# Two gated layers: order edges on the Sign activations and on the statistics of the next batch

## The chip, the cores and the metric

The kernel runs on one core of a Trainium2 chip. The metric is the device time of one execution in microseconds (us); the time before is a median of three executions.

## What is computed

The input is `x`, 4 batches of 512 tokens of width 512. Two layers follow one another, each of the same outer form:

```python
xn = layernorm(x)
x = x + attention(xn) * silu(ffn(xn))
```

In layer 0 the attention has 32 query heads of width 16 over 8 key heads, with a softmax over 512 keys; the ffn is a gated one, whose weights the kernel first multiplies with Hadamard matrices. In layer 1 the attention is a gated delta rule (a recurrence over the tokens, done in blocks), and the ffn uses only the signs of its weights:

```python
up_w, down_w = sign(up_weight), sign(down_weight)     # 2048x512, 512x2048
hidden = relu((x @ up_w.T) * up_scale)
out = (hidden @ down_w.T) * down_scale * output_scale
```

## The kernel before

**How an order comes about.** The source traces instructions engine by engine. A planner then writes each engine's stream at compile time: it plays the program through in a simulated time and lets, on each engine, the earliest instruction in the source's order go first among those that are ready in that simulated time. So an instruction whose inputs are ready early can stand far ahead of its place in the source. What a stream's order is once written, the engine follows: an instruction that waits holds back all behind it. The call `tc.keep_in_program_order(ins)` takes one piece of this freedom away: it adds an edge from the instruction that was traced last on the same engine to `ins`. The edge orders the two in the stream; it adds no semaphore and no wait.

**Layer 0.** One loop (`for u in range(NU + LATE)`, L529) runs over 256 units `u`, 64 for each batch. In unit `u` the attention does the row maxima of the scores of one pair of heads (`maxima`, two matmuls `sc` L402 on TensorE, one reduction `nmx` L403 on VectorE), and 11 units later the exponentials of the same pair (`exps`, two matmuls `st` L423, one activation `pe` L425 on ScalarE). There is one `sc` buffer and one `st` buffer (two PSUM banks each), so each unit's `st` matmuls wait until ScalarE has read the unit before, and each unit's `sc` matmuls until VectorE has. The ffn runs 16 units late (`v = u - 16`): of each 64 units the first 32 are the gate and up projections (`gate_up`, matmuls `mm` L316, then tanh L322 or a copy L326 on ScalarE), the other 32 the down projection (`down`, matmuls `y` L334). So gate_up stands in units 16 to 47, 80 to 111, 144 to 175 and 208 to 239, down in units 48 to 79 and so on. In batch 0 the weights are folded beside gate_up (`mix`, `fold`, `fold_down`; VectorE L52, L53, L247, L272); from batch 1 on they come back from memory, one 512 KB load `wc` (L312) for each unit, in 4 buffers.

**What else the loop places.** For the next batch: the load of `x` at unit 34 of each 64 (`load_x`, L128), four pairs `bn_stats`/`bn_aggr` at units 43 to 46 (`stats0`, L134 and L135), the standard deviation (`inv_std`, Sqrt L68 on ScalarE) and the normalization with its transposes at unit 49 (`norm0`, L73, L150 to L152). For layer 1: 32 tiles of weights, 256 KB each, are loaded into the three buffers `sn` (`load_weights`, L491 and L495, at units 100, 104, ... 224), turned into signs on ScalarE (`signs`, L498, at units 107, 111, ... 231) and stored to the memory tensor `sgn_d` (L499). Layer 1 reads `sgn_d` back from `load_signs` (L905) on.

```python
            if 100 <= u < 228 and u % 4 == 0:
                load_weights((u - 100) // 4)
            if 107 <= u < 235 and u % 4 == 3:
                signs((u - 107) // 4)
```

All DMAs of the loop are issued by one queue, SP's: `wc`, `sn`, `sgn_d`, `xin`, the small copies of queries (`qT` L389) and of the softmax denominators (`sum_d` L443, `rc` L445, `rec_d` L447, `sm` L450).

**Layer 1** begins after the attention's buffers are freed, some 818 us into the profiled execution.

Of the kernel before, what the change touches and what calls it, by code (L numbers as in the profile page):

```python
# [12 lines left out]
AF = mybir.ActivationFunctionType  # L13
# [20 lines left out]
def kernel(ctx: ExitStack, tc: tile.TileContext, i: dict, out: bass.AP):  # L34
    nc = tc.nc

    def new(pool, shape, dtype, tag, **kw):
        return pool.tile(shape, dtype, tag=tag, name=tag, **kw)
# [64 lines left out]
    if True:  # L103
# [20 lines left out]
        xins, xnTs, xrs = {}, {}, {}  # L124
# [5 lines left out]
        def stats0(b, t):  # L130
            if t == 0:
                lnp[b] = new(b0, [P, TB, 2], F32, "lnmv")
            s6 = new(b0, [P, 6], F32, "lnst")
            nc.vector.bn_stats(s6, xins[b][:, t, :])  # L134
            nc.vector.bn_aggr(lnp[b][:, t, :], s6)  # L135

        lnp = {}
# [79 lines left out]
        for t in range(TB):  # L217
            stats0(0, t)
# [276 lines left out]
                nc.sync.dma_start(sg, i["downT"][ts(c, P), :])  # L495

        def signs(n):
            nc.scalar.activation(sns[n], sns[n], AF.Sign)  # L498
            nc.sync.dma_start(sgn_d[n // 2, n % 2], sns[n])  # L499

        sns = {}
# [27 lines left out]
        for u in range(NU + LATE):  # L529
            b, r = u // 64, u % 64  # L530
# [30 lines left out]
            if 107 <= u < 235 and u % 4 == 3:  # L561
                signs((u - 107) // 4)
            if b + 1 < NB:
                if r == 34:
                    load_x(b + 1)
                if r in (43, 44, 45, 46):
                    stats0(b + 1, r - 43)
                if r == 49:
                    norm0(b + 1)
                if r == 52:  # L570
                    keys_values(b + 1)
# [712 lines left out]
    b = NB - 1  # L1284
# [20 lines left out]
    n = 0  # L1305
# [56 lines left out]
```

## Time and profile before

| | us |
|---|---|
| median of three executions | 1576.54 (1574.84 to 1581.1) |
| the profiled execution | 1569.52 |
| its span on the core | 1567.8 |
| TensorE busy / VectorE / ScalarE / GpSimd | 1474.4 / 1023.9 / 644.8 / 363.4 |
| mean granted TensorE clock | 0.978 |

The share of busy time is of the span. The page's 40 slices are 39.2 us each. In views of waits a row reads: who waited, on which line, for whom; then microseconds in total, how many times, and the longest. In a timeline a row reads: start, duration, engine, line, operation, tiles, shape, count, and in brackets the idle time before it and what ended it. An index of time that this document uses often is the unit: the k-th `nmx` reduction (L403) on VectorE is that of unit k, so its start says when unit k is reached. In the profiled execution unit 48 starts at 186.8 us, 80 at 286.5, 112 at 382.9, 144 at 471.0, 176 at 569.1, 208 at 657.2 and 240 at 750.1.

### The profile page before, as it was taken

To read this page: it belongs to the slowest core of one execution; us is meant where nothing else is said; L and a number is where in the kernel's file an instruction comes from. 1 tells how busy PE (TensorE), PEld (TensorE's weight loads), DVE (VectorE), ACT (ScalarE), POOL (GpSimd) and SP (SyncE) were. 2 spreads that over 40 slices of the span, in tenths; PEclk is the share of its full clock that TensorE was granted. 3 is DMA by queue.
4 is the path that set the end of the run, shared out by engine and by line. 5 is a ranking of instruction groups with operands and counts; after the bars stand their busy time and mean duration, and the time that the engine had idled before them with its cause. 6 is when DMAs were issued, how large, how long until landed. Compare 5 with 4: busy or idle time off the path is not lost.

```text
span 1567.8 us, 22716 instructions
## 1 busy us (share of the span) xinstructions
PE 1474.4 (94%) x8144; PEld 879.0 (56%) x8144; DVE 1023.9 (65%) x1805; ACT 644.8 (41%) x913; POOL 363.4 (23%) x354
## 2 busy tenths in 40 slices
PE   6999999999999999999998999998999999998896
PEld 2556533465335543456334666886578756875683
DVE  6899645765557655566517669568955897477553
ACT  4655655575446654466433423213231223121112
POOL 1112100322003210133101431154214521244023
PEclk9999999999999999999999999999999999999987
DMA  8856745375105631166014443424452435225513
GB/s 277 324 196 225 259 151 173 126 248 175 25 21 200 221 122 26 59 212 213 19 45 138 123 132 96 127 85 128 128 165 61 141 103 167 78 70 171 142 32 104
DMA packets 192512, 215.91 MB, mean 138 GB/s; under 512 B 66480, under 2 KB 129424, under 8 KB 191504
## 3 DMA queue, kind: packets, MB, share of 16 engines
q1 hardware_dynamic: 189648, 213.33, 43.0%
q10 hardware_dynamic: 2752, 1.14, 0.3%
q8 instruction: 64, 1.05, 0.3%
q14 instruction: 48, 0.39, 0.1%
HBM read 155.22 MB, written 54.58 MB: 134 GB/s over the span
## 4 chain that ended last, share of the span: by engine, by line
PE 64%; DVE 20%; DMA 7%; issue 3%; POOL 2%; ACT 2%; SPq 1%; POOLq 0%; ACTq 0%; DVEq 0%
PE y L334 14%; PE mm L316 10%; PE y L934 5%; PE ph L921 5%; PE sc L402 4%; PE pu L766 3%; PE pu L714 3%; DVE nmx L403 2%; PE po L435 2%; DVE UT L1023 2%; DVE sx L1019 2%; DVE yc L722 2%; PE mm L243 2%; PE pu L1120 2%; PE pu L1144 2%
## 5 line engine op out<-in xcount | busy, mean ns | idle before, releaser
L403 DVE TENSOR_REDUCE nmx<-sc 128x2 f32<-128x1024 f32 x256 | 312.3, 1220 | 151.4 <-PE st L423 128.0
L425 ACT ACTIVATE pe<-st 128x1024 f16<-128x1024 f32 x256 | 262.8, 1027 | 148.0 <-PE st L423 146.6
L334 PE MATMUL y<-wdn,hT 128*128 128x512 f32 x512 | 256.7, 622 | 4.9 <-DVE g L338 4.0
L316 PE MATMUL mm<-xr,wc 128*128 128x512 f32 x768 | 206.3, 409 | 0.9 <-DVE th L323 0.8
L316 PEld LDWEIGHTS mm<-xr,wc 128*128 128x128 f32 x768 | 136.8, 188 | 49.3 <-issue 21.3
L327 POOL TENSOR_TENSOR hT<-hT,th 128x512 f32<-128x512 f32 x64 | 83.6, 1306 | 320.6 <-ACT hT L326 260.9
L334 PEld LDWEIGHTS y<-wdn,hT 128*128 128x128 f32 x512 | 86.7, 190 | 93.0 <-issue 85.0
L714 PE MATMUL pu<-xn1T,wp 128*128 128x512 f32 x288 | 132.7, 604 | 0.0
L921 PE MATMUL ph<-xsh,sg 128*128 128x512 f32 x256 | 115.2, 450 | 0.8 <-ACT hT L926 0.8
L452 POOL TENSOR_TENSOR oT<-os,sm 128x512 f16<-128x512 f32 x32 | 41.3, 1292 | 318.0 <-DMA sm<-rec_d 264.9
L423 PE MATMUL st<-qm,kT 32*128 32x512 f16 x512 | 102.8, 386 | 7.2 <-ACT pe L425 7.2
L402 PE MATMUL sc<-kT,qT 32*128 32x512 f16 x512 | 102.3, 385 | 7.7 <-DVE nmx L403 7.5
L926 ACT ACTIVATE hT<-ph,upsc 128x512 f32<-128x512 f32 x64 | 43.8, 685 | 155.6 <-PE ph L921 152.1
L921 PE MATMUL ph<-xsl,sg 128*128 128x512 f32 x256 | 103.5, 404 | 2.0 <-DVE xsl L898 2.0
L934 PE MATMUL y<-sg,hsh 128*128 128x512 f32 x256 | 86.5, 447 | 5.6 <-DMA sg<-sgn_d 4.0
L323 DVE SCALAR_TENSOR_TENSOR th<-th,mm 128x512 f32<-128x512 f32 x64 | 43.6, 682 | 65.8 <-ACT th L322 65.7
L714 PEld LDWEIGHTS pu<-xn1T,wp 128*128 128x128 f32 x288 | 54.7, 195 | 55.7 <-issue 54.1
L402 PEld LDWEIGHTS <-qT 32*128 32x128 f16 x512 | 26.1, 91 | 100.1 <-issue 94.8
L934 PE MATMUL y<-sg,hsl 128*128 128x512 f32 x256 | 74.7, 405 | 0.0
L316 PE MATMUL mm<-xr,fo 128*128 128x512 f32 x256 | 71.7, 419 | 0.0
L322 ACT ACTIVATE th<-mm,hwg 128x512 f32<-128x512 f32 x64 | 44.1, 689 | 53.0 <-PE mm L316 52.0
L326 ACT COPY hT<-mm 128x512 f32<-128x512 f32 x64 | 37.5, 586 | 55.7 <-PE mm L316 55.7
(282 smaller groups left out, 2434.8 us busy)
## 6 DMA issues: line engine op xcount, KB each, us to landing
wc<-wS SPq DMA_DIRECT2D x96, 512.0 KB
sg<-sgn_d SPq DMA_DIRECT2D x128, 256.0 KB
wS<-fo SPq DMA_DIRECT2D x16, 1024.0 KB
sm<-rec_d SPq DMA_DIRECT2D x128, 64.0 KB
sgn_d<-sn SPq DMA_DIRECT2D x32, 256.0 KB
raw<-in_w_gateT SPq DMA_DIRECT2D x8, 512.0 KB
hT<-in_w_downT SPq DMA_DIRECT2D x16, 256.0 KB
raw<-in_w_upT SPq DMA_DIRECT2D x8, 512.0 KB
```

What stands on the lines that cost most here:

```text
L316: nc.tensor.matmul(pgs[m], wcs[b, c, m][:, h, k, :], xrs[b][:, k, :], start=(k + h == 0), stop=(k == KC - 1 and h == 1))
L322: nc.scalar.activation(th, pgs[0], AF.Tanh, scale=hwg[:, c : c + 1])
L327: nc.gpsimd.tensor_tensor(hT, hT, ths[b, c], ALU.mult)
L334: nc.tensor.matmul(ys[t], hTs[b, c][:, ts(t, P)], wdn[:, c, :], start=(c == 0), stop=(c == NI - 1))
L402: nc.tensor.matmul(sc[:, j, :], qTs[n][rows, ts(t, P)], kTs[b, g // 4][rows, :], start=True, stop=True)
L403: nc.vector.tensor_reduce(nmxs[n][:, t, 2 * pr : 2 * pr + 2], sc, AX.X, ALU.max, negate=True)
L423: nc.tensor.matmul(st[:, j, :], kTs[b, g // 4][rows, ts(k, P)], qms[n][rows, :], start=True, stop=True)
L425: nc.scalar.activation(pes[u], st, AF.Exp)
L714: nc.tensor.matmul(pp, wps[b, n][:, k, 0:P], xn1Ts[b][:, k, :], start=(k == 0), stop=(k == KC - 1))
L766: nc.tensor.matmul(pg[:, ts(t, n)], xn1Ts[b][:, k, ts(t0 + t, P)], wps[b, 9 + m][:, k, 0:n], start=(k == 0), stop=(k == KC - 1))
L921: ins = nc.tensor.matmul(ph, sgs[b, c, 0][:, ts(k, P)], xss[b][n][:, k, :], start=(k + n == 0), stop=(k == KC - 1 and n == 1))
L934: ins = nc.tensor.matmul(yss[b][t], hss[b, c][n][:, ts(t, P)], sgs[b, c, 1], start=(c + n == 0), stop=(c == NI - 1 and n == 1))
```

## The change

The `Sign` activation of each tile of layer 1's weights, and the `bn_stats` of the batches 1 to 3, each get an edge from the instruction traced before them on their engine. `bn_aggr`, the loads, the stores and batch 0's statistics get none. Nothing else is changed: no instruction is added or taken away.

```diff
             s6 = new(b0, [P, 6], F32, "lnst")
-            nc.vector.bn_stats(s6, xins[b][:, t, :])
+            ins = nc.vector.bn_stats(s6, xins[b][:, t, :])
+            if b > 0:
+                tc.keep_in_program_order(ins)
             nc.vector.bn_aggr(lnp[b][:, t, :], s6)
...
         def signs(n):
-            nc.scalar.activation(sns[n], sns[n], AF.Sign)
+            tc.keep_in_program_order(nc.scalar.activation(sns[n], sns[n], AF.Sign))
             nc.sync.dma_start(sgn_d[n // 2, n % 2], sns[n])
```

## The prediction

> **What bounds the kernel now.** I read the page first, then the waits of TensorE and ScalarE in the stretch where the signs run, then timelines around the longest wait, then the same for the statistics.
>
> ```profile
> span 1567.8 us, 22716 instructions
> PE 1474.4 (94%) x8144; PEld 879.0 (56%) x8144; DVE 1023.9 (65%) x1805; ACT 644.8 (41%) x913; POOL 363.4 (23%) x354
> ```
>
> TensorE is busy for 94%. So work moved between other engines is worth nothing by itself; only the 93 us in which TensorE stands still (and any time at a lower clock) can be won. Where do the two kinds of instruction that the change touches stand? By their starts, all 32 signs run from 145.6 to 266.3 us, that is in units 38 to 73, though the source has them in units 107 to 231 (368.6 to 726 us). The `bn_stats` of batch 1 run at 137.0 to 157.9 us (units 36 to 41; source 43 to 46), of batch 2 at 332.6 to 336.4 (unit 95; source 107 to 110), of batch 3 at 518.1 to 521.9 (unit 159; source 171 to 174). The planner put both far ahead. Did their inputs come in time? ScalarE's and TensorE's waits from 100 to 300 us:
>
> ```profile
> ACT sn L498 <- DMA sn<-in_upT: 12.9, 8, 3.3
> ACT sn L498 <- DMA sn<-in_downT: 6.6, 6, 2.3
> PE st L423 <- ACT pe L425: 5.7, 4, 3.4
> ```
>
> They did not: ScalarE stood 19.5 us in front of 14 signs, and TensorE stood 5.7 us for exponentials, its largest wait in this stretch. That one causes the other shows in the timelines of ScalarE and TensorE at the longest case:
>
> ```profile
> 224.75 0.63 ACT L498 ACTIVATE sn<-sn 128x512 f32<-128x512 f32 x1 [3.33 <-DMA sn<-in_upT]
> 226.36 0.63 ACT L498 ACTIVATE sn<-sn 128x512 f32<-128x512 f32 x1 [0.98 <-DMA sn<-in_downT]
> 226.90 0.57 ACT L442 COPY os<-po 128x512 f32<-128x512 f32 x1
> 227.36 1.03 ACT L425 ACTIVATE pe<-st 128x1024 f16<-128x1024 f32 x1
> ...
> 224.68 0.39 PE L402 MATMUL sc<-kT,qT 32*128 32x512 f16 x2
> 228.44 0.61 PE L423 MATMUL st<-qm,kT 32*128 32x512 f16 x2 [3.38 <-ACT pe L425]
> 228.98 3.78 PE L334 MATMUL y<-wdn,hT 128*128 128x512 f32 x4
> ```
>
> Two signs wait for loads, the exponential behind them starts at 227.36, and the next `st` matmuls need its buffer. The four `y` matmuls after the gap take 3.78 us; the same four take 1.98 at 233.79. VectorE's and TensorE's timelines at batch 3's statistics:
>
> ```profile
> 518.09 1.29 DVE L134 BATCH_NORM_STATS2 lnst<-xin 128x6 f32<-128x512 f16 x2 [2.48 <-DMA xin<-in_x]
> 519.51 0.68 DVE L134 BATCH_NORM_STATS2 lnst<-xin 128x6 f32<-128x512 f16 x1
> 520.69 1.22 DVE L403 TENSOR_REDUCE nmx<-sc 128x2 f32<-128x1024 f32 x1
> ...
> 521.96 0.39 PE L402 MATMUL sc<-kT,qT 32*128 32x512 f16 x2 [2.52 <-DVE nmx L403]
> ```
>
> The statistics wait 2.48 us for `x`, the row maximum stands behind them, and TensorE stands 2.52 us.
>
> **What the Trainium skill says.** TensorE: Matmul & The Clock Gate, "Architectural detail", has ScalarE's and VectorE's queues as strict FIFO; both timelines agree, since exponential and maximum start only after the instruction that waits. The same page, "What's actually happening", halves TensorE's clock after an idle window of about 3.4 us. The trace agrees: after 3.38 us matmul groups take 1.6 to 1.9 times as long until 233.8, after 2.52 us they don't. DMA: Bandwidth & Descriptors, "Anatomy of one DMA", has DMAs wait for semaphores on the sequencer that issues them, so a load of `sn` that waits for its buffer holds all of SP's queue; SP's waits show it (8.3 and 6.6 us for `sgn_d` stores from 100 to 300 us).
>
> **Signs, the gain.** TensorE's four gaps behind signs are 3.38, 0.39, 1.06 and 0.84: 5.7 us. The slow stretch: 3.78 - 1.98 = 1.8, and three steps of the small groups 0.22 longer each: 2.5 us. Sum **8.2**. A cross-check: the down phase with signs, units 48 to 80, lasts 99.7 us (186.8 to 286.5), those without 88.1 (382.9 to 471.0 and 569.1 to 657.2). Of the 11.6, 1.1 is the last `fold_down` at 187; 8.2 for the signs fits, and 2.3 I can't place.
>
> **Signs, the cost at the new place.** The predecessors are each unit's exponential or its `mm` copy, tied to TensorE's work, so the edge holds. The activations are spread, one in 4 units, about 11 us. Each takes 0.63 us, 0.53 in a row of others. In down phases ScalarE idles 1.2 us or more per unit, in gate_up 0.9: hidden, 0. If a sign stands right ahead of an exponential, `st` has about 0.9 us to spare, so 0 to 0.2 each; I take 0. Sixty-four DMAs of 256 KB (16.8 MB) move along, past SP's `wc`, `qT`, `rc` and `oTc` issues. Over 357 us they add 47 GB/s where phases now show 24 (down) and about 200 (gate_up). In down that is free. In gate_up stand 16 of the 32 signs. For each, SP issues a load and a store (0.40 and 0.39 us) and waits: 14.9 us in 29 reloads and 9.1 in 32 signs before, 0.8 each; together 1.6 us. What is queued behind is a `wc` load, issued 7 to 9 us ahead of its first matmul in most cases, but as little as 3.15 us (at 711.7), when TensorE's weight load just waited 0.2: a load needs about 3.1. So a hold of 1.6 us hurts where the lead is under 4.7, and with 0.85 us more for a load that shares the memory with 256 KB (at the 300 GB/s of the fullest slices) where it is under 5.5: 8 of the 64 `wc` loads from unit 144 on. The small row `rc` (L446) is exposed as well: VectorE waited 1.19 us for it at 375, and TensorE 1.36 behind it. Bounds: 0, if every lead covers it; 16 x 1.6 = 26 us, if none does. I take the share of short leads, 8/64 x 16 signs = 2 hits of about 1 us, and 1.5 for one more late `rc`: **3.5**.
>
> **Statistics.** For batches 2 and 3 `x` has landed by 332.6 and 518.1, and source units 107 and 171 come at 368.6 and 554.6: the wait (0.72 and 2.48) goes. Each pair of `bn_stats` and `bn_aggr` costs VectorE 0.7 us and falls into another unit, where VectorE idles 1 us or more. TensorE's gaps that go: 0.75 and 0.31 at 336 and 338, 2.52 and 0.83 at 520 and 524: **4.4**. Late next are Sqrt and `norm0`, which now follow unit 110. The two table loads of 1.28 us and the Sqrt just move; the transposes run at unit 114 before (387.9) and can still. For batch 1, 4 x 0.7 = 2.8 us leave the fold stretch (118 to 160 us: VectorE busy 41.1 of 42), but TensorE is busy 40.6 there, so at most 1.4 is to be won; I take 0.6. Its new place, 170 to 180 us, has VectorE at 14 of 20.
>
> **Sum.** 8.2 + 4.4 + 0.6 - 3.5 = 9.7, say **10 us**. Against the profiled execution's 1569.5 (span and 1.7 around it) that makes 1559.5. It lay 7.0 under the median; the same 10 off the median gives **1566.5**.
>
> **Rivals.**
> - *Given back (0.25).* SP's holds and the later `rc` eat most: 10 instead of 3.5 leaves 13.2 - 10 = 3, 1573.5. For it: the small leads, and a memory share already at 0.90 from 500 to 520 us. Against it: typical leads of 8 us, and that loads of `sn` have three buffers and 11 us per sign.
> - *Slower (0.10).* One mechanism: in gate_up, a `sn` reload that stands ahead of `wc` in SP's queue and waits for a store to land; about 3.1 us plus 0.8 of issue, of which TensorE loses 1.5 at each of 16 signs: 24 - 13.2 = 11 slower, 1587. It decides from 0.83 us per sign on (13.2 / 16). Before, the longest such wait was 6.6 us, but TensorE then had its weights in place.
> - *Nothing moves (0.05).* If the instruction before a sign or statistic in the source is itself placed early, the edge binds nothing: 1576.5. The predecessors' ties to TensorE speak against it.
> - Layer 1, from 818 us on, has the same work. A planner that starts it with other times may order it differently: I allow 5 us either way, for the range only.
>
> **Numbers.** Likeliest case 0.60, 1566.5, its own range 1556 to 1573. About 0.5%, 7.9 us, is what a measurement here can tell from no change; the case reaches over that line (1568.7) in most of its range, 0.53 of its 0.60; with 0.03 of the second, faster has 0.56. The rest of these two and the third make same 0.33; slower 0.11 is the third rival and an ill turn in layer 1. The range goes from all gain, no cost and a good layer 1 (13.2 + 5 + 1 off: 1557) to past no change, 1581.
>
> **What would show it.** Signs spread from about 360 to 715 us with no long wait for their loads; the gap of 3.38 us and the half clock gone, units 48 to 80 in about 90 us; statistics one per unit with no wait for `xin`; units 80 to 112 and 144 to 176 shorter by 1 and 3 us, less what signs cost in the second. It is wrong if `wc` or `rc` appear among TensorE's or VectorE's larger releasers after 370 us, or if units 208 to 240 take well over their 92.9 us; or if gains stand in layer 0 and layer 1 grows.

## The result and the profile after

The changed kernel takes **1586.09 us** (median of 13 runs), the kernel before 1574.84 beside it: a ratio of 1.0068, 95% interval 1.0051 to 1.0086. The forecast was 1566.5. The change is slower, by about 11 us. The profiled execution after took 1592.13 us, the longest of its 13, and the one before 1569.52, below its median; so differences between these two profiles overstate the loss by some 11 us. Every reading of a stretch of units below rests on one profile of each kernel.

The page of the changed kernel (its lines are shifted by 2 from L137 on, so `mm` is L318, `wc` L314, signs L500):

```profile
span 1590.4 us, 22741 instructions
PE 1488.4 (94%) x8144; PEld 887.6 (56%) x8144; DVE 1025.6 (64%) x1805; ACT 644.8 (41%) x913; POOL 363.8 (23%) x354
L318 PE MATMUL mm<-xr,wc 128*128 128x512 f32 x768 | 214.3, 422 | 9.4 <-DMA wc<-wS 9.4
```

The same line of the page before:

```profile
L316 PE MATMUL mm<-xr,wc 128*128 128x512 f32 x768 | 206.3, 409 | 0.9 <-DVE th L323 0.8
```

The counts of working instructions are the same on every engine, yet TensorE is busy 14 us longer and its `mm` matmuls take 422 ns in the mean where they took 409. The total is 25 higher (22741 against 22716): these are all semaphore instructions, 15 of them SP's. So an edge adds none by itself, but the new order of the streams did. The signs and the statistics by tile and by line:

```profile
L500 ACT ACTIVATE sn<-sn x32: 621/632/746, 357.9 to 744.7; 128x512 f32<-128x512 f32 x32
L134 DVE BATCH_NORM_STATS2 lnst<-xin x16: 634/683/694, 4.4 to 574.3; 128x6 f32<-128x512 f16 x16
```

The edges bind: the signs run from 357.9 to 744.7 us, one in four units, and no wait of ScalarE for a load of `sn` is left. TensorE's largest waits from 370 to 780 us, first after, then before:

```profile
PE mm L318 <- DMA wc<-wS: 9.4, 7, 3.0
PE sc L404 <- DVE nmx L405: 5.2, 7, 1.3
```

```profile
PE sc L402 <- DVE nmx L403: 5.5, 3, 2.5
```

A releaser that was not there has come to the top: the loads `wc`. The table gives the length of each stretch of units, from the starts of the `nmx` reductions, for every kernel of this document (one profiled execution each; gate_up in units 80 to 112, 144 to 176 and 208 to 240), with ratio to the kernel before from the timed runs.

| kernel | ratio (95% interval) | 0-48 | 48-80 | 80-112 | 112-144 | 144-176 | 176-208 | 208-240 |
|---|---|---|---|---|---|---|---|---|
| before | 1 | 166.2 | 99.7 | 96.4 | 88.2 | 98.1 | 88.1 | 92.8 |
| the change | 1.0068 (1.0051 to 1.0086) | 165.1 | 90.7 | 98.1 | 91.4 | 112.1 | 90.3 | 103.5 |
| e1 signs only | 1.0058 (1.0040 to 1.0075) | 165.7 | 90.4 | 97.8 | 90.1 | 108.4 | 90.2 | 103.5 |
| e2 statistics only | 0.9992 (0.9977 to 1.0007) | 169.0 | 99.4 | 95.8 | 90.5 | 95.8 | 88.6 | 94.2 |
| e3 GpSimd's queue | 0.9998 (0.9982 to 1.0013) | 165.5 | 91.2 | 98.0 | 89.5 | 101.7 | 89.1 | 99.8 |
| e4 down units | 0.9987 (0.9972 to 1.0003) | 166.2 | 91.4 | 95.3 | 96.1 | 97.4 | 94.6 | 93.8 |
| e5 reciprocal later | 1.0058 (1.0040 to 1.0075) | 164.6 | 90.6 | 94.6 | 89.2 | 107.2 | 90.6 | 107.5 |
| e6 = e4 + e5 | 0.9943 (0.9922 to 0.9965) | 166.1 | 90.4 | 95.7 | 92.7 | 94.7 | 94.8 | 94.8 |
| e7 five wc buffers | 1.0021 (1.0007 to 1.0035) | 169.6 | 90.9 | 95.0 | 91.6 | 106.5 | 90.2 | 99.5 |
| e8 = e3 + e5 | 0.9968 (0.9955 to 0.9981) | 165.4 | 90.3 | 93.8 | 89.1 | 98.5 | 89.2 | 98.6 |
| g1 = e3 + e4 + e5 | 0.9916 (0.9890 to 0.9941) | 165.5 | 90.5 | 93.6 | 91.2 | 93.8 | 90.7 | 94.7 |
| g3 wc on GpSimd's queue | 1.0164 (1.0138 to 1.0191) | 166.2 | 90.7 | 98.7 | 91.9 | 106.8 | 89.8 | 107.7 |
| g4 reciprocal alone | 0.9994 (0.9974 to 1.0014) | 169.1 | 98.9 | 97.5 | 87.7 | 98.8 | 87.5 | 94.2 |
| g5 gate_up units | 1.0236 (1.0209 to 1.0262) | 166.4 | 90.9 | 96.5 | 88.6 | 110.6 | 97.6 | 116.0 |
| h1 waits off SP | 1.0057 (1.0036 to 1.0078) | 165.5 | 91.3 | 92.3 | 89.1 | 110.1 | 88.4 | 105.0 |
| h2 an eighth of the bytes | 0.9958 (0.9943 to 0.9973) | 168.6 | 91.1 | 96.0 | 89.1 | 100.3 | 88.5 | 94.6 |
| h3 = g1, statistics free | 0.9969 (0.9952 to 0.9986) | 165.8 | 90.3 | 98.0 | 89.3 | 97.0 | 89.8 | 94.9 |

The 9 us in units 48 to 80 came as forecast. They are more than lost again in the two gate_up phases in which 14 of the signs now run: 14.0 and 10.7 us. From unit 240 on, most of it layer 1, the two profiles differ by 1.4 us only. How one such loss looks, in TensorE's timeline and in SP's, both of the changed kernel:

```profile
518.24 0.39 PE L425 MATMUL st<-qm,kT 32*128 32x512 f16 x2
521.64 2.89 PE L318 MATMUL mm<-xr,wc 128*128 128x512 f32 x8 [3.01 <-DMA wc<-wS]
524.46 0.61 PE L404 MATMUL sc<-kT,qT 32*128 32x512 f16 x2
```

```profile
507.56 0.38 SPq L314 DMA_DIRECT2D wc<-wS  x1
508.04 0.54 SPq L487 DMA_DIRECT2D xn_d<-xo  x1
510.83 0.31 SPq L449 DMA_DIRECT2D rec_d<-rc  x1
511.19 1.85 SPq L391 DMA_DIRECT2D qT<-qd  x3
513.14 0.58 SPq L487 DMA_DIRECT2D xn_d<-xo  x1
513.82 1.96 SPq L452 DMA_DIRECT2D sm<-rec_d  x4
515.82 0.53 SPq L391 DMA_DIRECT2D qT<-qd  x1
516.38 0.58 SPq L497 DMA_DIRECT2D sn<-in_downT  x1
517.42 0.34 SPq L314 DMA_DIRECT2D wc<-wS  x1
```

TensorE waits 3.01 us for a load that was issued only at 517.42, 9.9 us after the `wc` load before it. (The matmuls after the gap take 0.61 us where they took 0.39 before it: that is the half clock.) In between SP stood until 510.83 for the reciprocal of the softmax denominators, and then issued eight small transfers, `xn_d` and one reload of `sn`. The same two `wc` loads before:

```profile
511.18 0.53 SPq L312 DMA_DIRECT2D wc<-wS  x1
511.81 0.59 SPq L485 DMA_DIRECT2D xn_d<-xo  x1
512.44 0.62 SPq L128 DMA_DIRECT2D xin<-in_x  x1
513.25 0.52 SPq L447 DMA_DIRECT2D rec_d<-rc  x1
514.72 0.58 SPq L485 DMA_DIRECT2D xn_d<-xo  x1
515.39 0.57 SPq L312 DMA_DIRECT2D wc<-wS  x1
```

Here 4.2 us lie between the two `wc` loads. The windows of units 144 to 176, after and before, have as columns the window, its length, then busy time and count on TensorE, its weight loads, VectorE, ScalarE and GpSimd, then the granted clock, the DMA share and GB/s:

```profile
465.30:577.40 112.10, 101.95 (x503) 59.81 (x501) 62.84 (x92) 64.56 (x87) 29.37 (x24) 0.92 0.64 206
```

```profile
471.00:569.10 98.10, 92.19 (x503) 55.30 (x501) 64.17 (x95) 61.62 (x80) 28.36 (x23) 1.00 0.64 211
```

TensorE stands 10.2 us there against 5.9, and the same matmuls take 9.8 us longer. Most of that is the clock: for 17.1 us it was granted at half, which is worth at most 8.5. So in this stretch of this profile the lower clock costs more than the longer waits. That does not hold for the kernel as a whole: this is the slowest of its 13 executions. Span times (1 - granted clock), the most that a lower clock can have cost, is 40.2 us in the mean of all 13, and 36 to 38 us in each of the four sets of runs of the kernel before that stand beside the experiments. So in the balance the clock accounts for 2 to 4 of the 11 us. The mean DMA share of the stretch is the same 0.64; no average shows the cause.

### The profile page after: what moved, and what is told of

The parts are those of the page before. It is cut to its first block, busy times and chain, and to the rows that moved or that the text cites. A ratio compares the mean times of both kernels' runs of the same rounds, so it can differ in the third digit from the quotient of the medians.

```text
span 1590.4 us, 22741 instructions
## 1 busy us (share of the span) xinstructions
PE 1488.4 (94%) x8144; PEld 887.6 (56%) x8144; DVE 1025.6 (64%) x1805; ACT 644.8 (41%) x913; POOL 363.8 (23%) x354
## 4 chain that ended last, share of the span: by engine, by line
PE 64%; DVE 20%; DMA 7%; issue 3%; POOL 2%; ACT 2%; SPq 1%; POOLq 0%; ACTq 0%; DVEq 0%
PE y L336 14%; PE mm L318 10%; PE y L936 5%; PE ph L923 5%; PE sc L404 4%; PE pu L768 3%; PE pu L716 3%; DVE nmx L405 2%; PE po L437 2%; DVE UT L1025 2%; DVE sx L1021 2%; DVE yc L724 2%; PE mm L245 2%; DMA rc<-sum_d 2%; PE pu L1122 2%
## 5 line engine op out<-in xcount | busy, mean ns | idle before, releaser
L318 PE MATMUL mm<-xr,wc 128*128 128x512 f32 x768 | 214.3, 422 | 9.4 <-DMA wc<-wS 9.4
L318 PEld LDWEIGHTS mm<-xr,wc 128*128 128x128 f32 x768 | 142.7, 196 | 60.8 <-issue 21.8
L404 PE MATMUL sc<-kT,qT 32*128 32x512 f16 x512 | 105.0, 388 | 10.4 <-DVE nmx L405 10.0
L404 PEld LDWEIGHTS <-qT 32*128 32x128 f16 x512 | 26.7, 91 | 101.5 <-issue 97.5
L318 PE MATMUL mm<-xr,fo 128*128 128x512 f32 x256 | 71.2, 416 | 0.0
```

The lines of the kernel that those rows point to most:

```text
L318: nc.tensor.matmul(pgs[m], wcs[b, c, m][:, h, k, :], xrs[b][:, k, :], start=(k + h == 0), stop=(k == KC - 1 and h == 1))
L404: nc.tensor.matmul(sc[:, j, :], qTs[n][rows, ts(t, P)], kTs[b, g // 4][rows, :], start=True, stop=True)
```

## The experiments

Each is compared with the kernel before, run on the same chip; edits are against the changed kernel unless said otherwise.

**e1 and e2: which half?**

```diff
-            if b > 0:
-                tc.keep_in_program_order(ins)                                    # e1
-            tc.keep_in_program_order(nc.scalar.activation(sns[n], sns[n], AF.Sign))
+            nc.scalar.activation(sns[n], sns[n], AF.Sign)                        # e2
```

> The edge on the signs alone; the statistics are left free as before. Theory Q (the signs' loads and stores hold SP's queue in front of the wc loads in gate_up units): the loss is the signs', so 1582 to 1590 against 1575, with wc among TensorE's releasers in units 144 to 176 and 208 to 240 and the half clock after its gaps. Theory B (the bytes of the signs slow the wc loads, whoever issues them): the same. Theory S (the statistics, now late, cost it): about 1566, the gain of the signs alone.

> The edge on the statistics alone; the signs stay free, ahead in units 38 to 73. Theories Q and B: 1568 to 1574, the 4 us forecast for the statistics or less, no wc wait of TensorE. Theory S: 1585 or more.

Measured 1587.67 and 1575.77 us against 1577.69. The loss is the signs', and with their edge in place that on the statistics changes nothing either (1.0058 against 1.0068). The statistics alone change nothing that can be measured. What they win in units 80 to 112 and 144 to 176 (0.6 and 2.3 us) stands against 2.8 in units 0 to 48 and 2.3 in 112 to 144 of the profiles.

**e3: the signs' DMAs on another queue; e4: signs where no wc is loaded**

```diff
-                nc.sync.dma_start(...)      # the two loads of sn, the store of sgn_d
+                nc.gpsimd.dma_start(...)                                          # e3
-            if 100 <= u < 228 and u % 4 == 0:
-                load_weights((u - 100) // 4)
-            if 107 <= u < 235 and u % 4 == 3:
-                signs((u - 107) // 4)
+            if u in WL:                     # WS: 113, 115 ... 143, 177 ... 207   # e4
+                load_weights(WL.index(u))   # WL: each 5 less
+            if u in WS:
+                signs(WS.index(u))
```

> Both edges as in the change, but the 32 loads and 32 stores of the signs are issued by GpSimd's queue and not by SP's: the bytes and their times stay, SP's holds for them go. Theory Q: TensorE's waits for wc go, 1563 to 1570. Theory B: as the change, 1583 to 1590. A cost of its own is possible: GpSimd's products stand behind DMA issues that wait.

> Both edges as in the change, but the signs stand in the source in the down phases only: one in two units, 113 to 143 and 177 to 207, each load 5 units ahead. No wc load is due there but the four for the next phase. Theories Q and B: units 144 to 176 and 208 to 240 fall back to 98 and 93 us, in all 1562 to 1570. Theory S: as the change, 1583 to 1590. Denser signs may cost the down phases 1 to 3 us each.

Both come to the time before and no lower, and so lie between the forecasts of the theories: 1576.93 and 1575.10 against 1577.69. e3 takes 10 us off units 144 to 176 and 4 off units 208 to 240, as theory Q has it, but 3.6 and 7.0 stay. From 460 to 780 us TensorE waits less for `wc` than in the change, but VectorE waits longer for the denominators (9.7 us in 7 cases in the change):

```profile
PE mm L318 <- DMA wc<-wS: 3.7, 3, 2.3
DVE rc L448 <- DMA rc<-sum_d: 13.1, 11, 2.9
```

e4 cures gate_up and loses 7.9 and 6.5 us in the down phases, where 1 to 3 had been allowed for. VectorE's and TensorE's timelines in e4 show by what:

```profile
438.64 0.25 DVE L448 RECIPROCAL rc<-rc 128x16 f32<-128x16 f32 x1 [3.90 <-DMA rc<-sum_d]
440.03 0.39 PE L404 MATMUL sc<-kT,qT 32*128 32x512 f16 x2 [2.06 <-DVE nmx L405]
```

The reciprocal of the denominators waits 3.9 us for its load, and the next maximum, and so TensorE, behind it. That is a second place where time goes once the signs' DMAs stand beside it. It gave the next four runs.

**e5 to e8: two places, taken away singly and together**

```diff
-            nc.vector.reciprocal(rc, rc)                                          # e5
-            nc.sync.dma_start(rec_d[b, g]...
+            late.setdefault(at[0] + 2, []).append(lambda: quotients(b, g, os_, rc))
...
+        def quotients(b, g, os_, rc):      # called two units later
+            tc.keep_in_program_order(nc.vector.reciprocal(rc, rc))
+            nc.sync.dma_start(rec_d[b, g]...
...
-                    wcs[b, c, m] = new(zp[0], [P, 2, KC, P], F32R, "wc", bufs=4)
+                    wcs[b, c, m] = new(zp[0], [P, 2, KC, P], F32R, "wc", bufs=5)  # e7
```

e6 has this beside e4's edit, e8 beside e3's.

> As the change, but the reciprocal of the softmax denominators and all that follows it (rec_d, sm, oT, oTc) is traced two units later and the reciprocal is held in the source's order: VectorE no longer stands at it for the rc load. Theory W (what is lost in gate_up is TensorE's wait for wc and the half clock after it): nothing to gain, 1582 to 1588. Theory R (VectorE's wait for rc, 9.7 us in 7 cases from 460 to 780 us, is the larger part, as the maximum behind it feeds TensorE): 1570 to 1577.

> The signs in the down phases as in the run before this one, with the reciprocal two units later. There no wc load is hurt, and what is left is rc (10.4 us of VectorE in 3 waits from 370 to 470 us). Theory R for the down phases: the 14 us that units 112 to 144 and 176 to 208 lost fall to 3 or less, in all 1562 to 1568. If rc is only a symptom of a loss elsewhere: as before, 1573 to 1578.

> As the change, but with five buffers for wc in place of four: each load can be issued one unit (2.7 us) earlier. Theory W: the waits for wc and most of the half clock go, 1570 to 1577. Theory R: 1582 to 1588. If SP's queue is so full that an earlier free buffer gives no earlier issue: 1582 to 1588 as well, with the wc waits still there.

> The change with the signs' loads and stores on GpSimd's queue and the reciprocal two units later: both suspects removed. If W and R are all of it, the 9 us of units 48 to 80 stay and the later phases return to their lengths before: 1563 to 1569. If the bytes of the signs themselves slow wc: units 208 to 240 stay some 5 us long, 1570 to 1576.

Measured 1584.63, 1567.07, 1579.05 and 1569.74 us against 1575.25. e5: nothing is won with `wc` still late. Theory R is weakened by this, not refuted: two units later VectorE still waits for the load, 7.2 us in 9 cases from 370 to 780 us where it was 11.7 in 10, so the suspect was taken away only in part. e6: where `wc` is out of the way, the later reciprocal is worth 0.4%, and the kernel is faster than before. The down phases stayed at 92.7 and 94.8, not the 3 us loss or less that was expected. e7: a fifth buffer gives back two thirds of the loss, between the two forecasts. In its profile, the slowest of its 22 executions, TensorE still waits 10.3 us for `wc` from 370 to 780 us; that an earlier free buffer does not help while SP stands elsewhere fits this, but is not shown. e8: with both places relieved the gain shows, though units 208 to 240 keep 5.8 us; two waits for `wc` are left, one in each gate_up phase.

**g1, g3, g4, g5: the best of these, the converse, a control, the dose**

g1 is e3, e4 and e5 together. g3 moves `wc` in place of the signs; g4 is the kernel before with e5's edit; g5 is e4 with other units.

```diff
-                    nc.sync.dma_start(wcs[b, c, m].bitcast(F32), wS[c, m])
+                    nc.gpsimd.dma_start(wcs[b, c, m].bitcast(F32), wS[c, m])      # g3
-        WS = [*range(113, 145, 2), *range(177, 209, 2)]
+        WS = [*range(145, 177, 2), *range(209, 241, 2)]                           # g5
```

> The signs in the down phases, their loads and stores on GpSimd's queue, the reciprocal two units later, both edges kept. If what is left of the loss in the down phases (92.7 and 94.8 us against 88.1) is SP's hold of the denominators' small DMAs behind reloads: both phases back under 90 us, in all 1558 to 1564. If it is the bytes: 1565 to 1569, no better than with SP's queue.

> The change with one thing altered: the wc loads of batches 1 to 3 go through GpSimd's queue, the signs' loads and stores stay on SP's. The bytes and SP's holds stay, but wc no longer stands behind them. Theory Q: TensorE's waits for wc go, units 144 to 176 and 208 to 240 fall from 112 and 104 us to under 102 and 97, in all 1567 to 1576. Theory B, or if GpSimd's products hold wc as long as SP did: 1582 or more.

> A control: the kernel before, with the reciprocal two units later and neither edge. If the later reciprocal is worth nothing where the signs don't crowd it: 1572 to 1579, as before. If it brings the gain of the down-phase kernel by itself: 1565 to 1569.

> The dose turned up: both edges, all 32 signs in gate_up phases, one in two units (145 to 175 and 209 to 239), where the change has 14. Theory Q: the loss there, 10 to 14 us for 8 and 10.7 us for 6 signs, doubles or more: units 144 to 176 and 208 to 240 at 115 us or over each, 1595 to 1620 in all, while units 112 to 144 and 176 to 208 are back at 88 to 90. If the loss is a fixed cost of a new order and not of each sign: 1580 to 1590.

Measured 1560.65, 1600.92, 1573.63 and 1610.93 us against 1572.07. **g1** beats both kernels, by 0.8% against before. Its phases of down are 91.2 and 90.7: better than e6's, not quite under 90. From 460 to 780 us TensorE has no large wait left; the largest in total is

```profile
PE mm L414 <- DVE nm L411: 3.3, 4, 1.0
```

g4: the later reciprocal is worth nothing by itself. g5: 32 signs in gate_up cost 2.4%, the change's 14 there (and 2 more in units 80 to 112) cost 0.7%: the loss grows with their number. It is not even: units 144 to 176 did not grow with 16 for 8, units 208 to 240 more than doubled their excess, and units 176 to 208, where only the last two signs of a batch still run, took 9.5 us more than before. **g3** is the run whose forecast was most wrong. TensorE and VectorE from 460 to 780 us:

```profile
PE sc L404 <- DVE nmx L405: 18.3, 7, 4.6
```

```profile
DVE rc L448 <- DMA rc<-sum_d: 34.3, 11, 6.8
```

No wait for `wc` is left among TensorE's, as theory Q said, but VectorE now stands 34.3 us for the denominators, and TensorE behind it. Their round trip (defined below) did not become slower: 7.4 us in the mean of the same eight cases, 7.7 in the change. VectorE comes to the reciprocal sooner, since TensorE no longer holds it up, and in three cases because the planner put the reciprocal one maximum earlier in the stream. So with one wait relieved the other comes into the open: the two gate_up phases take as long as in the change (214.5 us in sum, 215.6 there). Of the 6.8 us by which the profile is longer than the change's, 5.5 lie after unit 240, and no run looks into that.

**h1 and h2: SP's waits or the bytes?**

```diff
-            nc.sync.dma_start(sgn_d[n // 2, n % 2], sns[n])
+        def store_signs(n):                 # at units 110, 114, ...              # h1
+            tc.keep_in_program_order(nc.sync.dma_start(sgn_d[n // 2, n % 2], sns[n]))
...
-                nc.sync.dma_start(sg, i["downT"][ts(c, P), :])
+                nc.sync.dma_start(sg[:, 0:64], i["downT"][ts(c, P), 0:64])        # h2
...
-            nc.sync.dma_start(sgn_d[n // 2, n % 2], sns[n])
+            nc.sync.dma_start(sgn_d[n // 2, n % 2, :, 0:64], sns[n][:, 0:64])
```

In h1 the two loads are held in order likewise, and in h2 the other load is cut the same way. h2 leaves seven eighths of layer 1's ffn weights without their sign: it is a probe of time and not a kernel to use.

> The change, with each sign's store traced 3 units after its sign, the reload 2 units after the store, and both held in the source's order on SP's queue: SP no longer stands in front of a store whose sign is still to come (20 us in 14 waits of the change) nor of a reload whose store has yet to land (19.7 us in 14). Bytes and issues stay. If those waits are the cause: units 144 to 176 and 208 to 240 at 102 and 97 us or less, 1566 to 1574 in all. If it is the bytes or the mere issues: within 4 us of the change, 1580 to 1588.

> The change with an eighth of the bytes: each of the 64 DMAs moves 64 of the 512 columns, into three standing buffers, and the rest of sgn_d is filled with the plain weights by 32 copies on GpSimd's queue at units 48 to 79, so layer 1's ffn works on weights that are mostly not signs. Issues and SP's order stay, landings are shorter. Looked at are units 144 to 176 and 208 to 240 only: if the bytes are the cause, under 100 and 95 us; if SP's holds and issues are, over 106 and 100.

Measured 1585.83 and 1570.16 us against 1575.46. SP's wait for signs from 460 to 780 us in the change:

```profile
SPq L501 <- ACT sn L500: 16.7, 10, 6.8
```

h1, TensorE's and SP's waits in the same window:

```profile
PE mm L318 <- DMA wc<-wS: 7.9, 3, 3.4
```

```profile
SPq L503 <- ACT sn L500: 7.0, 6, 2.4
```

SP's wait for signs fell from 16.7 us to 7.0, and the loss stayed. Counted over all stores and loads of the signs, SP stands 30.6 us at them in the change and 16.0 in h1: half, not all. TensorE also waits 7.9 us for exponentials in h1, where the change shows 0.4 us of this. h2, TensorE's and VectorE's:

```profile
PE mm L318 <- DMA wc<-wS: 5.8, 5, 2.0
```

```profile
DVE rc L448 <- DMA rc<-sum_d: 6.3, 9, 1.4
```

With all 64 issues in place and an eighth of their bytes, units 144 to 176 and 208 to 240 take 194.9 us in sum, against 215.6 in the change and 190.9 before: some 21 of the 25 us go, and the kernel is faster than before. Smaller transfers also land sooner, so SP stands less at the signs' DMAs, 16.4 us. But that is about what it stands in h1, where the two phases take 215.1 us: at the same standing, the bytes make a difference of 20. e3 moves all of the bytes by another queue, with none of this standing left on SP's, and there the two phases take 201.5 us: either the bytes cost less away from SP's queue, or the standing matters once all of it is gone. These runs do not separate the two. The round trip of the denominators, from the start of the `sum_d` issue to the start of the reciprocal, in the mean of the eight in those two phases: 6.4 us before, 7.7 in the change, 7.8 in e3, 8.4 in h1, 7.0 in h2.

**h3: the other half of the change, in the fastest kernel.** g1 without the edge on the statistics (e1's edit).

> The fastest kernel so far (signs in the down phases, GpSimd's queue, reciprocal later) without the edge on the statistics. If that edge is worth the 4 us forecast for it where nothing else crowds: 1564 to 1567, against 1560.7 with it. If it is worth nothing, as it was alone: 1559 to 1563.

Measured 1570.58 us against 1575.46, above both forecasts. The ratio is 0.9969 where g1 has 0.9916, each against the kernel before on its own chip, and the intervals do not meet: here the edge on the statistics is worth about 0.5%. In the profiles units 80 to 112 are 4.4 and 144 to 176 are 3.2 us shorter with it, units 112 to 144 and 176 to 208 1.9 and 0.9 longer.

## Why the prediction was wrong

**The signs' gain was right.** 8.2 us were forecast; units 48 to 80 shortened by 9.0, and by 8.3 to 9.4 in every kernel that moves the signs away. The gap of 3.38 us and the half clock after it are gone.

**The statistics' gain, 4.4 us, was right in place but not in the sum.** With the signs still early (e2) it is offset elsewhere; in the fastest kernel it shows, at 8 us or so, twice the forecast; what makes it twice was not looked into. The 0.6 us for the fold stretch came in none of the profiles clearly: units 0 to 48 were 1.1 us shorter in the change and 2.8 longer in e2.

**The step that failed is the cost at the new place: 3.5 us.** In the profiles the two gate_up phases lost 24.7 us and units 80 to 144 and 176 to 208 another 7. The forecast's own sign of being wrong came true: units 208 to 240 took 103.5 us. Three terms of the working were wrong.
- It took the leads of `wc` in the trace before as given, counted 8 short ones in 64, and gave each hit 1 us. But a lead is itself an outcome: it is what is left after SP has stood for other things. Counted in the same way, from the end of the issue, 15 leads are short in the change. The one at 517 us fell to 3.9 us from 10.3, after SP had stood for the reciprocal, and two more are at about 3 us near 720 and 750. TensorE's waits for `wc` came to 9.4 us in 7 cases, where 2 hits of about 1 us were priced.
- It called the down phases free. They lost 3.2 and 2.2 us, and with the signs twice as dense (e4) 7.9 and 6.5, of which VectorE's wait for `rc` is the visible part.
- It left out the clock. The text had just shown that a gap of 3.38 us was followed by half the clock; yet it priced gaps by their length alone. In units 80 to 240 of the profiles the change runs 30.7 us at half clock, and before had none there; over all executions this term is small, 2 to 4 us in the balance.

**The rival "slower" had the right place and nearly the measured time, but its mechanism was not confirmed; the match of the time is luck.** It put 24 us on `wc` behind reloads that wait for a store to land. SP's standing at the reloads is 12.4 us in the change, 8.0 in h1 and 5.0 in h2, over the same window. h1, with a third less of it, loses as much as the change; h2, with another 3 us less, loses 20 us less in the two phases. So the loss does not follow these waits, though no run takes them away alone. What e3, g5 and h2 show together is that the loss in the gate_up phases comes from the signs' DMAs on SP's queue, and goes for the most part with their bytes.

**How the bytes act is argued and not shown.** The timelines suggest a chain: 256 KB, in and out, ahead of or beside the small transfers, the round trip `sum_d`, `rc`, `rec_d` late, SP standing for it, `wc` issued late, TensorE waiting, then half the clock. In two of the eight round trips, those before the long gaps at 518 and 721 us, VectorE did stand at the reciprocal (1.9 and 3.1 us), and they took 8.5 and 9.3 us where both took 6.1 before. In the other six VectorE waits 0.2 us or less, so their lateness is as well a consequence of TensorE's gaps as a cause. And e3 speaks against the chain as the whole account: its round trips are as late as the change's, 7.8 us, yet its two phases lose 10.6 us and not 24.7.

The Trainium skill, DMA: Bandwidth & Descriptors, "Queues, rings and completion order", says that each DMA engine takes the rows of its queues in turn, and consumes what lies in one row in order. TensorE's waits for `wc` fit: with the signs on another queue they are 3.7 us against 9.4 from 460 to 780. VectorE's waits for `rc` do not follow so simply: they are 13.1 us in e3 against 9.7. No run here looks inside a DMA engine.

**What stays open**: by which of these links the bytes cost time, why units 208 to 240 keep 5.8 us in e8, and how much of g1's gain is the queue and how much the units, since the kernels differ in the planner's order as well, and one profile of each is at hand. (On top of e6 the queue takes the ratio from 0.9943 to 0.9916, with intervals that overlap; on top of e8 the units take it from 0.9968 to 0.9916.)

## What to carry to other kernels

Holding an instruction in its place takes the DMAs that feed and drain it along. Ask first what else lives on that queue at the new place, and count small round trips whose end something in order waits for, as well as the large loads: in e4, where no large load was hurt, such a round trip held VectorE for 3.9 us. A lead that a trace shows for a load is not a reserve that can be spent: short ones went from 8 to 15 here. And one wait can hide another, as g3 showed. g1 puts the background transfers where no stream of large loads runs, gives them a queue of their own and lets what waits for the small round trip stand a little later: with the same two edges it is 0.8% faster than the kernel before.

## What the runs showed of the hardware

The length of a gap did not decide whether TensorE's clock was halved. In the changed kernel 3.4 us of half clock followed a gap of 2.28 us that began at 363 us, and 13.7 us one of 3.01 that began at 518. The prediction read from the trace before that 3.38 us brought the half clock and 2.52 did not; both readings are right, but the same trace also has 3.4 us of half clock after a gap of 1.52 us that ended at 82.8, while the changed kernel has the same gap, ending at 82.3, at full clock. After the gap of 3.01 us, 13.7 us at half clock cost up to 7 us more, an estimate from half of that time.
